# A recurrence with side work between its steps: the period of the side work reordered over three periods, and its pieces dealt out by number

## The chip, the cores and the metric

The kernel runs on one core of a Trainium2 chip. Its time is the device time of one execution in microseconds (us); the value quoted for a kernel is the median of several executions. The profiled execution is one more execution, recorded instruction by instruction; its own time and its span (first to last instruction) stand beside the median in the table below.

## The reference

Two layers are applied to x of 16 x 512 x 256 (batch B, time T, channels C), each an attention-like part and a feed-forward part, each followed by a residual and a layernorm:

```
x = layernorm(x + attention(x))          # 16 heads, latent size 32, causal softmax
x = layernorm(x + fp4_feed_forward(x))   # 704 wide, inputs and weights rounded to a 4-bit grid
x = layernorm(x + recurrence(x))         # the stage of this change
x = layernorm(x + time_mix(x))           # and of this change
# recurrence, after an RMS norm to xn, per head (state 64, input 16):
state = tanh(state @ tanh(a) + xn_t @ b)
mixed = state @ c + skip * xn_t          # then tokens + mixed @ w_out + b_out
# time_mix: xk, xr = mixes of x_t and x_(t-1)
out = sigmoid(xr @ W_r) * (relu(xk @ W_k)**2 @ W_v)
```

The recurrence is serial over the 512 time steps; everything else is not.

## The kernel before

The first stage does attention and the fp4 feed-forward, batch by batch. It ends at about 1830 us of the span. The second stage (L830 onward) does recurrence and time mix. It is one loop over t = 0..511 (L1167 on, with the TensorE order written out by hand: the program order is the queue order on PE). The other engines' queues are ordered by the framework, roughly in the order in which the code issues the work.

A step t of the loop has a fixed part:

- `advance_state(0, t)` (L1051): 8 small matmuls on PE (L1060; the profile's rows count them as x8) of group 0's last state with tanh(a), accumulated on the inputs that already lie in the PSUM tile `u`, then two tanh on ACT (L1068), which write the new state into the ring `hist`.
- `make_inputs(t)` (L1151, its matmuls L1020): 8 matmuls of a later step's xn with b, into a `u` tile (three such tiles; a new one is begun at t%4==0).
- **slot A**: side work may be issued here.
- `advance_state(1, t)`: the same for group 1.
- at t%8==7, copies of the last eight states from `hist` into `c` (POOL L1194 and L1198, DVE L1201).
- **slot B**: side work may be issued here.

A group's matmuls of step t+1 need the tanh of its step t. The side work belongs to blocks of 16 steps x 16 batches (32 blocks). A block's side work is cut into generators, each resumed piece by piece (`step`, L1118):

- N (`normed`, 2 pieces): the first loads x, squares and sums on DVE (L859), and scales on POOL (L863 to L867), with nothing on PE; the second turns it by four PE transposes (L883, `ps_xn`) and stores xn on DVE (L872).
- R (`read_out`, 2 pieces): 8 matmuls each from `c` (L1036, `ro`), then DVE L1045 into `ot`.
- A (`out_of_recurrence`, 4 pieces of 4 matmuls, L904, `ps_a`): loads `xm` and adds the bias on POOL (L909); after the last piece DVE adds the residual (L921), takes the layernorm's sums (L91, L92), POOL makes the factor (L84, L86), and DVE scales in two halves (L891).
- M (`mixes`, 1 piece): four transposes of A's result (L883, `ps_x`), then on DVE a copy (L934), a difference (L938) and the two mixes (L942, `muk`, `mur`); POOL keeps the last token (L935, L933).
- K (`key`, 4 pieces of 4 matmuls, `ps_k`): reads `muk`; then DVE relu (L958), POOL square (L959).
- G (`gate`, 4 pieces, `ps_rr`): reads `mur`; then two tanh on ACT (L975).
- V (`value`, 4 pieces, `ps_kv`): reads K's and G's results, then DVE L990, L991, the sums, POOL's factor, DVE L891 into `o`, and two DMAs out (L999).
- D (feed-forward of the last batch, 7 pieces, only in periods 0 and 1).

Each generator takes one of two PSUM banks for its products (`mm`), which is free again when its reader on DVE or ACT is done.

`PERIOD` is the order of a period of 16 steps; the number is the block's distance from the period (K-2 in period M works on block M-2). `TIME` holds a cost for each letter. The pace is the sum of the period's costs divided by 15.5; slot A of each step adds 0.3 of it to a budget and slot B 0.7, and pieces are issued while the budget is above zero. With these numbers a full period of 21 pieces falls out like this (slot A | slot B, "-" is empty; N0 and N1 are N's two pieces):

```
0 K0|N0 K1   1 -|K2   2 K3|G0   3 -|G1   4 -|G2   5 G3|R0   6 -|R1   7 -|A0
8 -|A1   9 A2|A3   10 -|N1   11 -|V0   12 V1|-   13 M|-   14 V2|V3   15 -|-
```

After t = 511 the work that is left of the last blocks runs without the recurrence ("the end").

Of the kernel before, what the change touches and what calls it, by code (L numbers as in the profile page):

```python
# [59 lines left out]
def tile_kernel(ctx: ExitStack, tc: tile.TileContext, I: dict, out: bass.AP):  # L60
# [196 lines left out]
    def vector_step():  # L257
        if vector_work:
            if next(vector_work[0][1], True):
                vector_work.pop(0)  # L260
# [80 lines left out]
    with ExitStack() as a:  # L341
# [319 lines left out]
        def step(name, args):  # L661

            if (name, args) not in tasks:
                tasks[name, args] = TASKS[name](*args)
            return next(tasks[name, args])

        def plan(b):
            todo = []
            for entry in {0: PLAN_0, 1: PLAN_1, B - 1: PLAN_15}.get(b, PLAN):
                c, *rest = entry[1:].split(".")  # L670
                todo.append((entry[0], (b + int(c), *map(int, rest))))
            return todo


        TIME = {"L": 0.86, "H": 1.7, "V": 0.9, "O": 0.9, "Q": 0.0, "U": 1.7, "D": 1.65, "W": 0.82, "P": 0.5}

        class Beside:
            def __init__(self, b):
                self.todo = plan(b)
                self.pace = sum(TIME[n] for n, _ in self.todo) / (4 * len(BLOCKS) * 8)  # L680
                self.left = 0.0
# [104 lines left out]
        with tc.manual_schedule(engines={mybir.EngineType.PE}):  # L786
            slots = [(b, g, n) for b in range(B) for g in range(4) for n in range(len(BLOCKS))]
            pTs, before, beside = [], None, None

            behind = []  # L790
            for slot in slots + [None]:
                if slot:
                    b, g, n = slot
                    if g == 0 and n == 0:
# [4 lines left out]
                        beside = Beside(b)  # L799
# [212 lines left out]
    def inputs(u, g, t0, n):  # L1012

        for k in range(2):
            for par in range(2):
                at = (t0 - g * 4) % RING + par
                for half in range(2):
                    for r in range(2):
                        rs, bs = slice(r * 64, r * 64 + 64), half * 32 + r * 16
                        nc.tensor.matmul(  # L1020
                            u[rs, k, par:n:2, bs : bs + 16],
                            wb[:, g * 2 + k, par, half, rs], xt[:, g, at : at + n - par : 2, :],
                            start=par == 0 and half == 0, stop=False, skip_group_check=True,
                        )
                yield
# [25 lines left out]
    def advance_state(g, t):  # L1051
        t0, _, u = us[g]
        if state[g] is not None:

            for k in range(2):
                own = state[g][:, k, :].rearrange("p (r s b) -> p r s b", r=2, s=2)
                into = u[:, k, t - t0, :].rearrange("p (s r b) -> p s r b", s=2, r=2)
                for c in range(2):
                    cs = slice(c * 64, c * 64 + 64)
                    nc.tensor.matmul(  # L1060
                        into[cs, :, c, :], ta[:, t % 2, g * 2 + k, cs], own[:, :, c, :],
                        start=False, stop=True, skip_group_check=True,
                    )
        state[g] = hist[g][t // 8 % 2][:, t % 8, :, :]
        with tc.high_priority():
            for r in range(2):
                rs = slice(r * 64, r * 64 + 64)
                nc.scalar.activation(  # L1068
                    state[g][rs, :, r * 32 : r * 32 + 32].rearrange("p k (s b) -> p k s b", s=2),
                    u[rs, :, t - t0, :]  # L1070
                    .rearrange("p k (s r b) -> p k s r b", s=2, r=2)[:, :, :, r, :],
                    AF.Tanh,
                )

    def beside(M):

        todo = [("N", 1)] * 2 if M == 0 else []
        for e in PERIOD:
            i = M + int(e[1:])
            if 0 <= i < T // TS:  # L1080
                todo.append((e[0], i))
        return todo + LATER.get(M, [])
# [1 line left out]


    PERIOD = [
        "K-2", "N2", "K-2", "K-2", "K-2", "G-2", "G-2", "G-2", "G-2", "R-1", "R-1", "A-1", "A-1",
        "A-1", "A-1", "N2", "V-2", "V-2", "M-1", "V-2", "V-2",
    ]


# [10 lines left out]
        ],  # L1102
    }

    TIME = {
        "E": 0.0, "F": 0.0, "N": 0.3, "K": 0.46, "G": 0.46, "R": 0.5, "A": 0.46, "V": 0.46, "M": 0.6,
        "U": 0.6, "D": 0.47,
    }
    KIND = {
        "N": normed, "K": key, "G": gate, "R": read_out, "A": out_of_recurrence, "V": value, "M": mixes,  # L1110
        "U": lambda j: ffn_up(B - 1, j), "D": lambda j: ffn_down(B - 1, j),
# [13 lines left out]
    with tc.manual_schedule(engines={mybir.EngineType.PE}):  # L1125
        for e in FIRST:
            end = False
            while not end:
                step(e[0], int(e[1:]))
                end = ends[0]  # L1130
        banks[:] = [ps_2]
        five.close()
        ps_u = ctx.enter_context(tc.tile_pool(name="ps_u", bufs=3, space=PSUM))

        copier[0] = nc.vector.tensor_copy
        product_of[0] = by_64
        us, ahead = [None, None], {}

        starts = [
            [(t0, 8) for t0 in range(0, T, 8)],  # L1140
            [(0, 4)] + [(t0, min(8, T - t0)) for t0 in range(4, T, 8)],
        ]
        pieces = []
        for g in range(2):
            for t0, n in starts[g]:
                for q in range(4):
                    pieces.append((t0 - 4 + q, g, t0, n))
        pieces.sort(key=lambda e: (e[0] if e[2] else -9, e[1], e[2]))
        making = {}

        def make_inputs(until):  # L1151
            while pieces and pieces[0][0] <= until:
                _, g, t0, n = pieces.pop(0)
                if (g, t0) not in making:
                    u = ps_u.tile([P, 2, 8, 64], F32, tag="u", name="u")
                    making[g, t0] = (u, inputs(u, g, t0, n))
                next(making[g, t0][1])

        todo, left, pace = [], 0.0, 0.0

        def some(more):
            nonlocal left
            left += more
            while left > 0 and todo:
                left -= step(*todo.pop(0))

        for t in range(T):  # L1167
            if t % 16 == 0:
                for e in todo:
                    step(*e)  # L1170
                todo, left = beside(t // 16), 0.0
                pace = sum(TIME[n] for n, _ in todo) / 15.5
                for g in range(2):
                    clean[t // 16, g] = histc.tile([P, 16, 2, 2, B], F32, tag=f"c{g}", name=f"c{g}")
            if t == 0:
                make_inputs(-1)
            for g in range(2):
                if us[g] is None or us[g][0] + us[g][1] == t:
                    t0, n = starts[g].pop(0)
                    us[g] = t0, n, making.pop((g, t0))[0]  # L1180
            vector_step()
            advance_state(0, t)
            make_inputs(t)
            some(pace * 0.3)
            advance_state(1, t)
            if t % 8 == 7:
                at = t % 16 - 7
                for g in range(2):
                    old, new = hist[g][t // 8 % 2], clean[t // 16, g]
                    old = old.rearrange("p t k (r s b) -> p t k r s b", r=2, s=2)  # L1190
                    for r in range(2):
                        rs, qs = slice(r * 64, r * 64 + 64), slice(64 - r * 64, 128 - r * 64)

                        nc.gpsimd.tensor_copy(  # L1194
                            new[rs, at : at + 8 : 2].rearrange("p t k s b -> p t k (s b)"),
                            old[rs, 0::2, :, r].rearrange("p t k s b -> p t k (s b)"),
                        )
                        nc.gpsimd.tensor_copy(  # L1198
                            new[rs, at + 1 : at + 8 : 2, :, r, :], old[rs, 1::2, :, r, r, :]
                        )  # L1200
                        nc.vector.tensor_copy(  # L1201
                            new[qs, at + 1 : at + 8 : 2, :, r, :], old[rs, 1::2, :, r, 1 - r, :]
                        )
            some(pace * 0.7)
        for e in todo:
            step(*e)
        for M in range(T // 16, T // 16 + 4):
            for e in beside(M):
                step(*e)
# [91 lines left out]
```

## Time and profile before

| what | value |
|---|---|
| median of 3 executions | 2583.96 us (2583.03 to 2585.3) |
| profiled execution, its own time | 2582.77 us |
| its span | 2581.0 us |
| mean granted TensorE clock | 0.983 |
| first state tanh (L1068) starts | 1830.4 us |
| last state tanh starts | 2549.1 us |

The second stage is thus the last 750 us of the span, 719 us of them the loop. In the profile's rows a matmul on PE has a weight load on PEld ahead of it; a row such as `L1060 MATMUL u<-hist,ta ... x8` is one `advance_state`. A number in brackets at the end of a row is the time that the engine was idle before it, with what ended the idle time. Times are us from the span's start, unless marked ns.

The start of every 64th L1068 row (4 per step, 16 steps) marks the periods. Period 0 takes 28.83 us, period 1 27.79, period 2 22.19, periods 3 to 29 take 22.08 on average (596.14 together), period 30 22.08, and the 15 steps of period 31 that are followed by another step 20.97.

### The profile page before, as it was taken

What the parts mean: (1) busy time and instruction counts of PE and PEld (TensorE: products, weight loads), DVE (VectorE), ACT (ScalarE), POOL (GpSimd) and SP (SyncE); (2) the same over time, 40 slices, a digit from 0 to 9 for tenths busy, and PEclk for the clock granted to TensorE, in tenths of its full rate; (3) what the DMA queues carried; (4) which work ended last, traced back from release to release, by engine and by line L of the source; (5) the groups of instructions that cost most, each with busy time, mean ns of one, the idle gap of its engine ahead of it and who ended that gap; (6) DMA issues with size and microseconds to landing.
All of it is one profiled execution on the core that took longest, in us unless ns stands there. A gap on an engine that the chain in (4) does not pass through costs nothing.

```text
span 2581.0 us, 73861 instructions
## 1 busy us (share of the span) xinstructions
PE 2438.0 (94%) x28802; PEld 1715.8 (66%) x28802; DVE 1946.9 (75%) x5621; ACT 1615.6 (63%) x5532; POOL 1048.2 (41%) x1649
## 2 busy tenths in 40 slices
PE   8789999999999999999999999996899999999997
PEld 4456666666666666666666666664677777777775
DVE  6767888787887888878888788887566666666665
ACT  4656666666666666666666666753366666666663
POOL 4322333333333333333333333333555555555653
PEclk9899999999999999999999999998899999999999
DMA  3000000000000000000000000000101111111100
GB/s 118 22 10 5 22 13 16 13 15 16 19 14 16 15 12 23 14 16 15 12 24 14 15 15 4 15 14 9 49 29 40 37 38 40 40 38 37 35 28 22
DMA packets 58016, 61.30 MB, mean 24 GB/s; under 512 B 7873, under 2 KB 53058, under 8 KB 57666
## 3 DMA queue, kind: packets, MB, share of 16 engines
q1 hardware_dynamic: 56802, 55.54, 6.9%
q8 instruction: 226, 3.70, 0.6%
q10 hardware_dynamic: 864, 1.05, 0.1%
q14 instruction: 124, 1.02, 0.1%
HBM read 39.79 MB, written 16.78 MB: 22 GB/s over the span
## 4 chain that ended last, share of the span: by engine, by line
PE 58%; DVE 27%; ACT 7%; POOL 4%; issue 3%; DMA 0%; ACTq 0%; POOLq 0%; DVEq 0%; SPq 0%
PE u L1060 7%; PE ps_pt L559 6%; PE S L524 5%; DVE p L536 5%; PE u L1020 4%; PE pg L160 4%; PE pu L160 3%; PE py L590 3%; ACT p L549 3%; PE ps_h L439 3%; PE ps_d L160 2%; PE ps_a L904 2%; PE ps_k L904 2%; ACT pT L561 2%; PE ps_q L457 2%
## 5 line engine op out<-in xcount | busy, mean ns | idle before, releaser
L549 ACT ACTIVATE p<-p,nm 128x512 f32<-128x512 f32 (+3 forms) x1024 | 569.7, 561 | 520.8 <-DVE nm L536 516.7
L1068 ACT ACTIVATE hist<-u 64x64 f32<-64x64 f32 x2048 | 447.3, 218 | 250.8 <-PE u L1060 182.5
L536 DVE CUSTOM_DVE_ANT_0 p<-S,mask 128x512 f32<-128x512 f32 (+3 forms) x1024 | 443.7, 483 | 50.1 <-PE S L524 50.1
L559 PEld LDWEIGHTS ps_pt<-ident,p 128*128 128x128 f32 x2560 | 296.7, 141 | 235.5 <-issue 86.2
L1060 PEld LDWEIGHTS u<-hist,ta 128*64 128x64 f32 x8176 | 362.9, 138 | 121.0 <-ACT hist L1068 41.6
L559 PE MATMUL ps_pt<-ident,p 128*128 128x128 f32 x2560 | 393.6, 280 | 9.2 <-DVE nm L536 3.5
L561 ACT COPY pT<-ps_pt 128x384 f32<-128x384 f32 (+1 forms) x768 | 370.3, 515 | 38.9 <-PE ps_pt L559 38.6
L1060 PE MATMUL u<-hist,ta 128*64 128x32 f32 x8176 | 384.2, 219 | 4.8 <-ACT hist L1068 4.5
L214 POOL TENSOR_TENSOR q_q<-q_q,q_m 128x256 f32<-128x256 f32 (+1 forms) x142 | 168.7, 1188 | 457.0 <-DVE q_q L213 442.7
L524 PE MATMUL S<-kc,qr 32*128 32x128 f32 (+3 forms) x2048 | 235.7, 474 | 8.9 <-ACT qr L478 7.9
L1020 PE MATMUL u<-xt,wb 128*64 128x64 f32 x4128 | 223.2, 230 | 3.5 <-issue 2.4
L549 ACT ACTIVATION_READ_ACCUMULATOR p<-p,nm 128x1 f32 x1024 | 198.9, 194 | 0.0
L160 PE MATMUL pg<-wgT,xqT 128*128 128x352 f32 x512 | 177.5, 470 | 4.2 <-ACT xqT L289 2.9
L473 POOL TENSOR_TENSOR qc<-qc,qs 128x512 f32<-128x512 f32 x64 | 81.6, 1275 | 236.0 <-DVE qs L472 230.9
L160 PE MATMUL pu<-wuT,xqT 128*128 128x352 f32 x512 | 172.5, 459 | 1.2 <-DVE th L304 1.2
L160 PE MATMUL ps_d<-wdT,hT 128*128 128x256 f32 x732 | 169.5, 381 | 2.2 <-ACT hT L323 2.2
L1020 PEld LDWEIGHTS u<-xt,wb 128*64 128x64 f32 x4128 | 165.0, 139 | 9.4 <-issue 3.0
L590 PEld LDWEIGHTS py<-pT,vpad 128*32 128x32 f32 x5120 | 141.2, 110 | 43.2 <-issue 30.7
L590 PE MATMUL py<-pT,vpad 128*32 128x128 f32 x5120 | 165.3, 276 | 3.8 <-ACT pT L561 3.5
L524 PEld LDWEIGHTS S<-kc,qr 32*128 32x128 f32 x2048 | 111.0, 185 | 78.2 <-issue 32.0
L160 PEld LDWEIGHTS ps_d<-wdT,hT 128*128 128x128 f32 x732 | 134.8, 191 | 19.6 <-ACT hT L323 3.1
L84 POOL TENSOR_SCALAR ve<-mv 128x1 f32<-128x1 f32 (+1 forms) x160 | 32.8, 205 | 264.5 <-DVE mv L92 234.7
(164 smaller groups left out, 4620.4 us busy)
## 6 DMA issues: line engine op xcount, KB each, us to landing
xT<-in_xT_dram SPq DMA_DIRECT2D x16, 512.0 KB
x<-in_x_dram SPq DMA_DIRECT2D x16, 512.0 KB
xs<-x SPq DMA_DIRECT2D x64, 128.0 KB
x<-xs SPq DMA_DIRECT2D x32, 256.0 KB
xm<-xs SPq DMA_DIRECT2D x32, 256.0 KB
out_dram<-o SPq DMA_DIRECT2D x64, 128.0 KB
w<-in_w_down_dram SPq DMA_DIRECT2D x2, 352.0 KB
w<-in_w_gate_dram SPq DMA_DIRECT2D x5, 128.0 KB
```

The source lines that it names most:

```text
L160: nc.tensor.matmul(dst, left, right, start=start, stop=stop)
L214: nc.gpsimd.tensor_tensor(q, q, m, ALU.subtract)
L524: nc.tensor.matmul(S[h][:, at : at + w], q[rs, i * P : i * P + P], k[rs, :w], start=True, stop=True,)
L536: nc.vector.tensor_tensor_reduce(out=p[:, own], in0=S[h][:, own], in1=mask[:, T - (i + 1) * P :], scale=1.0, scalar=-MASKED, op0=ALU.add, ...
L549: nc.scalar.activation(p[:, own], p[:, own], AF.Exp, bias=nm[:, u : u + 1], scale=-1.0, accum_out=sum_of[b, g][:, cb, half, h : h + 1],)
L559: nc.tensor.transpose(ps[:, at : at + P], p[:, at : at + P], ident)
L561: nc.scalar.copy(pT[:, :w], ps[:, :w])
L590: nc.tensor.matmul(py[q * 32 : q * 32 + 32, PLACE[i][1], :], vpad[b % 2][:, j, g * 4 + h, :], pt, start=j == 0 and h % 2 == 0, stop=j == i ...
L904: nc.tensor.matmul(dst[cs], left[:, cs], right, start=first, stop=not first)
L1020: nc.tensor.matmul(u[rs, k, par:n:2, bs : bs + 16], wb[:, g * 2 + k, par, half, rs], xt[:, g, at : at + n - par : 2, :], start=par == 0 an ...
L1060: nc.tensor.matmul(into[cs, :, c, :], ta[:, t % 2, g * 2 + k, cs], own[:, :, c, :], start=False, stop=True, skip_group_check=True,)
L1068: nc.scalar.activation(state[g][rs, :, r * 32 : r * 32 + 32].rearrange("p k (s b) -> p k s b", s=2), u[rs, :, t - t0, :] .rearrange("p k ( ...
```

## The change

The order of the period changes, V moves from two to three blocks behind, and the costs in `TIME` are gone: pieces are counted. At step k of a period of n pieces, `left` is n - n*(k+1)//16; slot A issues pieces while more than left + 1 remain, slot B until `left` remain. `step` returns N's first piece as 0.0, so that `piece` goes on behind it, if the count allows.

```diff
     PERIOD = [
-        "K-2", "N2", "K-2", "K-2", "K-2", "G-2", "G-2", "G-2", "G-2", "R-1", "R-1", "A-1", "A-1",
-        "A-1", "A-1", "N2", "V-2", "V-2", "M-1", "V-2", "V-2",
+        "N2", "V-3", "V-3", "V-3", "V-3", "K-2", "K-2", "R-1", "R-1", "K-2", "K-2", "A-1", "A-1",
+        "A-1", "A-1", "G-2", "G-2", "G-2", "G-2", "N2", "M-1",
     ]
...
-        todo, left, pace = [], 0.0, 0.0
-
-        def some(more):
-            nonlocal left
-            left += more
-            while left > 0 and todo:
-                left -= step(*todo.pop(0))
+        todo, number = [], 0
+
+        def piece(left):
+
+            while len(todo) > left and not step(*todo.pop(0)):
+                pass
...
-                todo, left = beside(t // 16), 0.0
-                pace = sum(TIME[n] for n, _ in todo) / 15.5
+                todo = beside(t // 16)
+                number = len(todo)
...
             make_inputs(t)
-            some(pace * 0.3)
+
+            left = number - number * (t % 16 + 1) // 16
+            while len(todo) > left + 1:
+                piece(left + 1)
             advance_state(1, t)
...
-            some(pace * 0.7)
+            piece(left)
```

A full period now falls out like this:

```
0 -|N0   1 -|V0   2 -|V1   3 V2|V3   4 -|K0   5 -|K1   6 R0|R1   7 -|K2
8 -|K3   9 A0|A1   10 -|A2   11 -|A3   12 G0|G1   13 -|G2   14 -|G3   15 N1|M
```

Period 2 has no V yet (17 pieces), periods 30 and 31 have no N (19 pieces), and period 1 has 16 pieces: N0, R0, R1, A0 to A3, N1, M, D0 to D6, one to a step. Period 0 has N0 and N1 of blocks 1 and 2 and fourteen D pieces; before, those four N pieces stood in slot A of steps 0 and 1, and now they stand in slot B of steps 0 to 3. In the order of the PE queue, behind the last step's matmuls, now stand M of block 30, V29, half of K30, R31, the rest of K30, A31, G30, M31, V30, K31, G31, V31; before, K30, G30, R31, A31, half of V30, M31, the rest of V30, K31, G31, V31.

More of the change, by code (lines that the diff above doesn't have):

```diff
@@ L1102, in tile_kernel @@
         ],
[L1103 to L1107, printed above, removed]
     }
```

## Prediction

> **What bounds the kernel now.** I read the page first, then the busy time by stretches of the second stage, then the waits of PE inside the loop, then the timeline of single periods.
>
> ```profile
> span 2581.0 us, 73861 instructions
> PE 2438.0 (94%) x28802; PEld 1715.8 (66%) x28802; DVE 1946.9 (75%) x5621; ACT 1615.6 (63%) x5532; POOL 1048.2 (41%) x1649
> ...
> 1830.00:1859.00 29.00, 25.25 (x485) 20.95 (x483) 14.90 (x41) 13.90 (x64) 22.16 (x33) 0.82 0.15 43
> 1859.00:1887.00 28.00, 23.38 (x468) 18.95 (x466) 13.34 (x38) 14.10 (x66) 11.32 (x29) 0.88 0.09 26
> 1909.00:2505.00 596.00, 584.31 (x12748) 471.38 (x12744) 401.33 (x1033) 395.23 (x1782) 344.15 (x752) 1.00 0.13 38
> 2549.00:2581.00 32.00, 16.89 (x130) 9.69 (x126) 18.29 (x46) 1.61 (x6) 8.64 (x17) 0.80 0.09 25
> ```
>
> The stretches' columns are length, then busy time of PE, PEld, DVE, ACT, POOL, the granted clock, the DMA share and GB/s. In the full periods (1909 to 2505) PE is busy 98% at full clock; periods 0 and 1 and the end have PE holes and a low clock. So a change of order can win only what is left of PE's waits. In 1909 to 2505 PE waits, by name, for this:
>
> ```profile
> PE ps_x L883 <- DVE x L891: 7.0, 21, 0.6
> PE u L1060 <- ACT hist L1068: 4.0, 26, 0.2
> ```
>
> The first is M waiting for A's layernorm. Period 17 (from 2218.62) has the wait, period 18 (from 2240.76) has not:
>
> ```profile
> 2231.41 0.63 PE L904 MATMUL ps_a<-woutT,ot 128*64 128x256 f32 x4
> 2235.27 1.70 DVE L891 TENSOR_SCALAR x<-x,mv,rstd 128x256 f32<-128x256 f32 x2 [0.80 <-POOL rstd L86]
> 2235.44 1.38 POOL L909 TENSOR_TENSOR xm<-xm,bout 128x512 f32<-128x512 f32 x1 [0.20 <-DMA xm<-xs]
> 2236.30 0.44 PE L883 MATMUL ps_x<-ident,x 128*128 128x128 f32 x2
> 2237.02 0.44 PE L883 MATMUL ps_x<-ident,x 128*128 128x128 f32 x2 [0.29 <-DVE x L891]
> ...
> 2257.41 0.74 DVE L891 TENSOR_SCALAR x<-x,mv,rstd 128x256 f32<-128x256 f32 x2 [0.68 <-POOL rstd L86]
> 2258.41 0.66 PE L883 MATMUL ps_x<-ident,x 128*128 128x128 f32 x4
> 2259.22 1.28 POOL L909 TENSOR_TENSOR xm<-xm,bout 128x512 f32<-128x512 f32 x1 [1.85 <-DMA xm<-xs]
> ```
>
> In period 17 POOL's L909 starts before the second half of L891, and the two halves take 1.70 instead of 0.74 us; M's second half waits. In period 18 L909 comes later, M's four transposes run together. Period 17 takes 22.14 us, period 18 takes 21.61: M's wait costs **0.53**. Periods 8, 11, 21 and 25 are like 18 (21.61 each), period 28 nearly (21.71), the rest of 3 to 29 like 17 or longer; their mean is 22.08.
>
> **The change, part by part.** *Work per step.* From the starts of PE's rows in period 17: an advance of a group holds PE 0.20, the inputs 0.26, a product piece 0.44 to 0.47. So a step without a piece is 0.67 of PE work, with one 1.12, with two 1.56. By the starts of L1068 the step with one piece in slot B takes 1.13 and with two 1.55 to 1.57 (PE's work), but the empty step 15 takes 1.05: there the chain advance, tanh, advance is the limit, and 0.37 is lost. R, N and M hold PE 0.24 to 0.27 longer than a product. The new full period has again five steps with two pieces, ten with one, and one without PE work (step 0 in place of step 15). The count therefore buys **nothing** in a full period: same rows, same holes. A new `u` tile costs about 0.17 at steps 4 and 12 in both orders, since slot B of the step ahead is full in both.
>
> *M's wait.* A3 to M was 4.9 us (2231.41 to 2236.30). Now slot B of step 11 to slot B of step 15 is steps 12 (1.56 + 0.17), 13 and 14 (1.13 each) and N1 ahead of M in step 15 (0.67 + 0.7 + 0.17 for the rest): 5.6 us. A's chain needs 5.6 in the slow form (2231.41 to 2237.02) and 4.6 without L891's excess of 0.96. L909 is now queued on POOL between the history copies of steps 14 and 15, behind A's factor (L86), so it cannot hold L891. M's data wait goes: 22.08 becomes 21.61.
>
> *What is late next: M's bank.* In the new order M takes the bank that G has just left, one step earlier, and so waits for G's second tanh. The nearest rows are these of period 16:
>
> ```profile
> 2203.04 0.60 PE L904 MATMUL ps_rr<-wrT,mur 128*64 128x256 f32 x4
> 2203.69 0.38 ACT L975 ACTIVATE th<-ps_rr 128x256 f32<-128x256 f32 x1 [0.17 <-PE ps_rr L904]
> 2203.97 0.51 ACT L1068 ACTIVATE hist<-u 64x64 f32<-64x64 f32 x2
> 2204.51 0.39 ACT L975 ACTIVATE th<-ps_rr 128x256 f32<-128x256 f32 x1
> ```
>
> The second tanh ends 1.86 after G3's start. From G3's start to M: 0.44 + 0.20 + 0.26 + 0.7 (N1) + 0.3 = 1.9. So between 0 and one more state pair (0.5) if that gets ahead; I take 0.05, as the rows' order on ACT is the same in the new program (tanh, state pair, tanh). Behind M on PE stands the next step's advance, so this wait would be paid in full. Full periods 3 to 29: 27 x (22.08 - 21.66) = **-11.3**.
>
> [...] Around steps 15 and 0 POOL now has eight history copies (0.35 to 0.45 each), L909 (1.28) and the carry, and on DVE at the same time stand M's difference and mixes and N's squares, and K0 waits for the first mix. [...] By the rows the loss is smaller: L942's pair took 1.20 beside L867 at 2239.02 and 0.87 in the quiet end, L938 1.22 beside L909 at 2259.83 and 0.69 elsewhere. [...] I take the rows: cost nothing. Other slacks are larger: R1 to A0 3.4 us for 1.5 of work, K3 to G0 4.2 for 1.4, A3 to N1 4.9 for 1.4, V3 to R0 (bank) 3.2 for 1.4.
>
> *N0's and V's queues.* N0's load, V's two output DMAs and `xm`'s load keep their order of one each a period on SP, and `x` and `xm` are loaded a period or more ahead; no wait there reaches PE. V one block later holds th, ka and x three buffers deep at most; the reuse is ten steps away.
>
> *Period 0.* N1's transposes waited for POOL's xn in slot A of steps 0 and 1 (3.2 us on PE, 1832 to 1837). xn comes at the same time, but PE then stands in step 3, two steps further: two bare steps (1.34) and the two empty steps 9 and 15 (0.75) fall away. **-2.1**, between 0 and -4.
>
> *Period 1* (27.79). M waits for A's factor, which POOL makes behind history copies:
>
> ```profile
> 1873.55 1.08 PE L883 MATMUL ps_x<-ident,x 128*128 128x128 f32 x4 [3.94 <-DVE x L891]
> ```
>
> After it the clock is 0.53 (stretch 1873 to 1879). The new period adds up to 1.05 (N0) + 2 x 1.39 (R) + 10 x 1.13 + 1.5 (D0's transposes) + 2 x 1.41 (N1, M) + 0.33 = 19.8, and waits of 0.7 (R on copies), 0.5 (D1 on hT) and about 2.5 for M, since A3 and M now stand a step later against the copies of step 7, which are further done when M asks. At full clock 23.5. [...] By the rule 23.5, by the row 25.5. I take between: **-3.0** (0 to -4.5).
>
> *Period 2* has four V pieces less: 4 x 0.44 and M's wait, **-2.3**. *Periods 30 and 31*: no N, no empty step, no wait of M (0.6 and 1.3 there): about 20.4 against 22.08, and 18.6 + 0.4 against 20.97 for what stands ahead of the last state: **-1.6, -2.0**.
>
> *The end* gets M30, V29 and half of K30 more. They lie in the 5 us in which R31 waits for the history copies and DVE anyway (it started 5.0 after the last advance); M30's chain puts R31 at about 5.5. After A31 G30 fills PE, and L990 no longer stands between d and `muk`, so 0.7 comes back. **-1.0** (-2 to +1.5).
>
> Sum: -2.1 - 3.0 - 2.3 - 11.3 - 1.6 - 2.0 - 1.0 = -23.3. The profiled execution's own time is 2582.77 (span 2581.0, 1.8 around it): 2559.5. The median lies 1.2 above that execution: **2560.7**.
>
> **Rivals.** *The wait is handed on (0.12).* M waits for G's tanh by a state pair more, 0.45 in each of 27 periods: the gain there is gone and about 12 remain from the edges: 2572. For it: G3 to M is one step where 1.9 is needed and 1.9 is there. Against: ACT is 66% busy.
>
> *K0 waits for `muk` (0.05), slower.* [...]
>
> *The change acts only at the edges and not on M (0.06)*, because A's chain is slow again in the new place: -12 and some loss, 2572 to 2579.
>
> *The edges give more (0.10)*: full clock in periods 0 and 1, 2553.
>
> **How the numbers follow.** The likeliest case (0.67) is 2560.7, its own range 2554 to 2568. The range 2552 to 2575 takes in the handed-on wait and the better edges, and leaves out the slower rival. About 0.2% (5 us) is what a measurement of this kernel can tell from no change. Faster by more: 0.67 + 0.12 + 0.10 and half of the third rival (0.03), less 0.03 of the likeliest for steps misjudged: 0.89; within: the other half and 0.02 of these, 0.05; slower: 0.05 and 0.01, 0.06.
>
> **What would show it.** Right: no row in periods 3 to 29 with M waiting for L891; periods of 21.6 to 21.7; L891 at 0.74 for its two halves everywhere; period 2 under 20. [...] It would be most wrong if a full period had a wait that I placed under a slack.

## The result, and the profile after

The changed kernel takes 2561.18 us (median of 4 runs, 2558.65 to 2561.73), the kernel before 2583.49 beside it (2581.19 to 2585.3): a ratio of 0.9912, 95% interval 0.99 to 0.9924. The forecast was 2560.7. The profiled execution of the changed kernel took 2558.65 with a span of 2556.6, against 2582.77 and 2581.0 before.

The head of the changed kernel's page:

```profile
span 2556.6 us, 73922 instructions
PE 2428.8 (95%) x28802; PEld 1713.3 (67%) x28802; DVE 1944.7 (76%) x5621; ACT 1613.2 (63%) x5532; POOL 1036.7 (41%) x1649
```

Its busy time by stretches, which are periods 0, 1, 3 to 29, and the end; columns as before (length, busy PE, PEld, DVE, ACT, POOL, granted clock, DMA share, GB/s):

```profile
1829.00:1855.00 26.00, 23.08 (x482) 19.09 (x479) 18.55 (x42) 13.49 (x62) 21.41 (x34) 0.93 0.17 48
1855.00:1881.00 26.00, 22.79 (x463) 18.59 (x462) 13.39 (x37) 14.15 (x66) 10.99 (x28) 0.87 0.10 28
1901.00:2486.00 585.00, 580.70 (x12758) 472.03 (x12756) 395.00 (x1036) 393.80 (x1782) 337.13 (x752) 1.00 0.13 38
2525.00:2557.00 32.00, 19.00 (x176) 11.40 (x172) 21.59 (x53) 3.35 (x13) 10.08 (x21) 0.90 0.09 25
```

The full periods are 11 us shorter at nearly the same count of PE rows, and PE is busy 99% of them. What PE still waits for in 1901 to 2486:

```profile
PE u L1060 <- ACT hist L1068: 4.1, 27, 0.2
PE ps_x L883 <- ACT th L975: 0.2, 1, 0.2
```

M's 21 waits for L891 are gone; the state's wait, one in each period (the step without a piece), is what it was. One M of 27 shows a wait for G's second tanh. The neighbourhood of M in one full period of the changed kernel (start, length, engine, line, operation; in brackets the idle time ahead and what ended it):

```profile
2222.43 0.73 DVE L891 TENSOR_SCALAR x<-x,mv,rstd 128x256 f32<-128x256 f32 x2 [1.09 <-POOL rstd L86]
...
2223.97 1.27 POOL L909 TENSOR_TENSOR xm<-xm,bout 128x512 f32<-128x512 f32 x1
...
2223.98 0.66 PE L883 MATMUL ps_xn<-ident,xn 128*128 128x128 f32 x4
2224.25 1.41 DVE L1199 COPY c<-hist 64x128 f32<-64x128 f32 x2 [1.09 <-ACT hist L1068]
2224.49 0.38 ACT L975 ACTIVATE th<-ps_rr 128x256 f32<-128x256 f32 x1
...
2224.92 0.66 PE L883 MATMUL ps_x<-ident,x 128*128 128x128 f32 x4
```

A's layernorm (L891) is through at 2223.16 with two halves of 0.73 together, 1.76 ahead of M. POOL's bias add L909 comes 0.8 after it. It now lies beside a history copy on DVE instead: two L1199 take 1.41, where their median is 0.31 each; nobody on PE asks for that copy then, and the DVE work queued behind it reaches PE in time. G's second tanh ends at 2224.87 and M starts at 2224.92, 0.05 behind it; in all 27 full periods it is 0.05 to 0.07.

Where the span's 24.4 us went, by the starts of every 64th L1068 (us; the three columns on the right are experiments told below):

| stretch | forecast | before | changed | difference | order alone | before, no bias add | changed, no bias add |
|---|---|---|---|---|---|---|---|
| up to the first state | 0 | 1830.37 | 1829.62 | -0.75 | 1832.18 | 1830.71 | 1831.33 |
| period 0 | -2.1 | 28.83 | 26.15 | -2.68 | 27.61 | 24.82 | 25.06 |
| period 1 | -3.0 | 27.79 | 25.62 | -2.17 | 27.12 | 27.84 | 24.14 |
| period 2 | -2.3 | 22.19 | 19.91 | -2.28 | 20.74 | 21.60 | 19.92 |
| periods 3 to 29 | -11.3 | 596.15 | 584.79 | -11.36 | 583.88 | 583.55 | 585.26 |
| period 30 | -1.6 | 22.08 | 21.19 | -0.89 | 21.26 | 22.06 | 20.70 |
| period 31 | -2.0 | 20.97 | 18.38 | -2.59 | 19.77 | 20.95 | 18.39 |
| the end | -1.0 | 32.62 | 30.92 | -1.70 | 30.18 | 30.63 | 30.93 |

### The profile page after: what moved, and what is told of

Same layout as the page of the kernel before. It is cut to its first block, busy times and chain, and to the rows that moved or that the text cites. A ratio compares the mean times of both kernels' runs of the same rounds, so it can differ in the third digit from the quotient of the medians.

```text
span 2556.6 us, 73922 instructions
## 1 busy us (share of the span) xinstructions
PE 2428.8 (95%) x28802; PEld 1713.3 (67%) x28802; DVE 1944.7 (76%) x5621; ACT 1613.2 (63%) x5532; POOL 1036.7 (41%) x1649
## 3 DMA queue, kind: packets, MB, share of 16 engines
q10 hardware_dynamic: 864, 1.05, 0.1%
## 4 chain that ended last, share of the span: by engine, by line
PE 54%; DVE 28%; ACT 9%; POOL 5%; issue 3%; DMA 1%; ACTq 0%; DVEq 0%; POOLq 0%
PE u L1060 8%; DVE p L536 6%; PE ps_pt L559 5%; PE u L1020 5%; PE S L524 4%; ACT p L549 4%; PE py L590 3%; PE pg L160 3%; PE pu L160 3%; PE ps_h L439 3%; ACT pT L561 3%; DVE q_q L207 2%; PE ps_a L904 2%; PE ps_d L160 2%; DVE q_sc L201 2%
## 5 line engine op out<-in xcount | busy, mean ns | idle before, releaser
L1068 ACT ACTIVATE hist<-u 64x64 f32<-64x64 f32 x2048 | 445.5, 218 | 235.1 <-PE u L1060 153.0
L1060 PE MATMUL u<-hist,ta 128*64 128x32 f32 x8176 | 394.2, 218 | 4.6 <-ACT hist L1068 4.4
```

What stands on the lines that cost most here:

```text
L1060: nc.tensor.matmul(into[cs, :, c, :], ta[:, t % 2, g * 2 + k, cs], own[:, :, c, :], start=False, stop=True, skip_group_check=True,)
L1068: nc.scalar.activation(state[g][rs, :, r * 32 : r * 32 + 32].rearrange("p k (s b) -> p k s b", s=2), u[rs, :, t - t0, :] .rearrange("p k ( ...
```

## The experiments

The theory: in the old order POOL's L909 lies beside A's layernorm, L891 is held, and M waits for it; the new order takes M and L909 out of each other's way, and the dealing by number brings nothing in a full period. The rivals: the dealing evens the steps and carries the gain; or M simply stood too near to A, with L909 a bystander.

**The order alone.** The kernel before with only this edit:

```
-        "K-2", "N2", "K-2", "K-2", "K-2", "G-2", ... "N2", "V-2", "V-2", "M-1", "V-2", "V-2",
+        "N2", "V-3", "V-3", "V-3", "V-3", "K-2", "K-2", "R-1", "R-1", ... "G-2", "N2", "M-1",
```

> The new order of the period, dealt out by the old rule of costs and pace. M then stands in slot B of step 14, A's last piece in slot B of step 9, G's last in slot B of step 12, and the step without a piece is step 15 as before. Theory (the order takes M away from A's chain, the dealing is worth nothing in a full period): M's wait for L891 is gone, full periods of 21.6 to 21.7 as in the changed kernel, time 2559 to 2566, the spread being the edges, where the two dealings put the pieces differently. Rival (the dealing by number carries the gain, for it evens the steps): full periods stay at 22.0 to 22.1, time 2575 to 2583.

Measured: 2564.68, ratio 0.9924 (0.991 to 0.9938). Full periods of 21.61, no M row waiting. The order carries the whole gain of the full periods (583.88, even 0.9 under the changed kernel). Periods 0, 1, 2 and 31 are 1.46, 1.50, 0.83 and 1.39 longer than in the changed kernel, the end 0.74 shorter: the dealing by number is worth some 4 us in this order, and at the edges only. (This is read from the periods of two profiled executions; the intervals of the two ratios overlap.)

**The dealing alone.** The changed kernel with the old `PERIOD`.

> The old order of the period, dealt out by number. M stands in slot B of step 14 and A's last piece in slot B of step 11: from the one to the other are about 3.8 us, where A's chain needs 4.6 without a hold and 5.6 with one. Theory: M waits for L891 0.8 to 1.8 in every period and its restart adds to it, full periods of 22.4 to 23.4, time 2592 to 2620, slower than before. Rival (the dealing by number carries the gain): full periods under 22.0, time under 2578.

Measured: 2626.77, ratio 1.0164 (1.015 to 1.0177): slower than before, and by more than expected. The sign was right and the wait was the wrong one. The profile shows no gap ahead of M: L891's halves take 0.41 or less, from A's last piece to M go 4.4 and not the 3.8 expected, and M starts at most 0.2 before the second half ends. It is K0 that waits. The waits of PE in its full periods (us in total, times, longest), and then the rows of one period:

```profile
PE ps_k L904 <- DVE muk L942: 32.5, 24, 1.7
PE u L1060 <- ACT hist L1068: 0.3, 1, 0.3
```

```profile
2161.88 0.66 PE L883 MATMUL ps_x<-ident,x 128*128 128x128 f32 x4
2162.69 0.68 DVE L934 COPY x3T<-ps_x 128x512 f32<-128x512 f32 x1
2163.10 1.27 POOL L909 TENSOR_TENSOR xm<-xm,bout 128x512 f32<-128x512 f32 x1
2163.40 1.05 DVE L1199 COPY c<-hist 64x128 f32<-64x128 f32 x1
2164.49 0.77 DVE L938 TENSOR_TENSOR d<-x3T 128x512 f32<-128x512 f32 x1
2165.29 0.31 DVE L1199 COPY c<-hist 64x128 f32<-64x128 f32 x1
2165.63 0.94 DVE L942 SCALAR_TENSOR_TENSOR muk<-d,cols,x3T 128x256 f32<-128x256 f32 x2
...
2166.20 0.65 PE L904 MATMUL ps_k<-muk,wkT 128*64 128x256 f32 x4 [1.28 <-DVE muk L942]
```

M has moved to step 14 and K0 is the first piece of step 0, 3.0 us behind it; from M's start to K0's, which stands right behind the first half of `muk` that it asks for, go 4.3. In that chain stands one history copy that L909 holds to 1.05 instead of 0.31; these 0.74 are the larger part of the 1.28 that K0 waits here, and the rest is the short distance itself. My expectation counted M's distance to A and forgot to count K0's to M. So the wait that the forecast named as its slower rival exists where the distance is too short, 1.35 each time. What the other DVE instructions between M and K0 take longer is at most a small part of it: L938 takes 0.77 here against 0.69 elsewhere, L859 0.61 against 0.42. The changed kernel has 6.34 from M to K0 (2224.92 to 2231.26 in the period shown above), and K0 does not wait.

A full period of the dealing alone takes 23.82, 1.7 more than before, and a part of that is the clock: in seven of the 27 periods the granted clock falls to 0.50 for 3.41 us behind K0's wait, and these periods take 24.9 to 25.1, the others 23.0 to 23.8.

**The kernel before without the bias add**, and **the changed kernel without it**: one line taken out of each, so that the output bias is missing from the result.

```
-        nc.gpsimd.tensor_tensor(x, x, bout.unsqueeze(1).to_broadcast([P, 2, C]), ALU.add)
```

> The kernel before without POOL's bias add L909: the output bias is left out of x. Order and dealing are untouched. Theory (L909 beside L891's second half holds it, and that alone makes M wait in the old order): L891 takes 0.4 each everywhere, no M row waits for it in the full periods, periods of 21.6 in place of 22.1, about 21 x 0.53 = 11 less: 2572 to 2574. Rival (M simply stands too near to A's chain in the old order, and L909 is a bystander): the wait and the 22.1 stay, 2581 to 2584.

> The changed kernel without L909, the output bias left out as in the kernel before without it. Theory: in the new order L909 holds nothing that PE waits for, so full periods stay at 21.6 to 21.65 and the time within 1.5 of the changed kernel, 2560 to 2562. If L909 still cost the new order something in period 1 or at the end, it would show as 2 to 3 us less there.

Measured: 2565.96 (0.9926, 0.9913 to 0.9938) and 2558.23 (0.9898, 0.9883 to 0.9913). What the rows of L891 for `x` look like in the full periods of before, of before without L909, and of the changed kernel (durations in ns: least, median, greatest), in this order:

```profile
L891 DVE TENSOR_SCALAR x<-x,mv,rstd x54: 401/415/1487, 1925.8 to 2500.2; 128x256 f32<-128x256 f32 x54
```

```profile
L891 DVE TENSOR_SCALAR x<-x,mv,rstd x54: 405/412/415, 1921.6 to 2483.9; 128x256 f32<-128x256 f32 x54
```

```profile
L891 DVE TENSOR_SCALAR x<-x,mv,rstd x54: 407/410/416, 1919.3 to 2482.8; 128x256 f32<-128x256 f32 x54
```

One POOL instruction, taken out of a kernel whose order is untouched, takes the long halves of 1.49 away, and with them M's wait: full periods of 21.60, 12.6 less over 27 of them, a little more than the new order brings. The bystander theory is out. And the two do not add up: in the new order L909 is worth nothing in the full periods (585.26 against 584.79). Both the new order and the missing add remove one and the same wait. The rest of the first kernel's gain (6 to 8 us more than expected) lies in period 0 (-4.0), period 2 (-0.6) and the end (-2.0). In period 0 L909 costs in another way: before, two of them stand on POOL for 2.50 us, from 1823.73, ahead of the xn that N's transposes wait for, and without them these waits fall from 3.2 to 1.2. The changed kernel without the add is 3.0 under the changed kernel's 2561.18, but the intervals of the two ratios overlap, and the changed kernel run once more (below) took 2558.11; in the profiled executions period 1 is 1.5 and period 0 1.1 shorter than in the first trace of the changed kernel, period 1 only 0.9 than in the second (25.05). The expectation had allowed for period 1 alone.

**A third tanh.** To see what the 0.05 between G's second tanh and M are worth, the changed kernel with that tanh issued twice:

```
         for i in range(2):
             nc.scalar.activation(th[:, i, :], ps[:, i * C : i * C + C], AF.Tanh, scale=0.5)
+        nc.scalar.activation(th[:, 1, :], ps[:, C : 2 * C], AF.Tanh, scale=0.5)
```

> The changed kernel with G's second tanh issued twice (one more ACT instruction of 0.38 in each period, the same result). In the changed kernel M started 0.05 after that tanh's end, in the bank that it frees. Theory (the wait is handed on to the tanh as soon as these 0.05 are gone, and is paid in full since the next step's advance stands behind M): M waits 0.3 to 0.35 in each full period and restarts for up to 0.2 more, 27 x 0.33 to 0.55 = 9 to 15 more, 2570 to 2576. Rival (the bank's release is not what M stands at, or the hole of the step behind takes the wait up): no M row that waits for the tanh, 2560 to 2564.

Measured: 2563.6 (0.9933, 0.992 to 0.9947). The wait is there as worked out, in every period:

```profile
PE ps_x L883 <- ACT th L976: 7.8, 27, 0.3
PE u L1061 <- ACT hist L1069: 4.2, 27, 0.2
```

One of them, by its rows:

```profile
2232.00 0.38 ACT L976 ACTIVATE th<-ps_rr 128x256 f32<-128x256 f32 x1
...
2232.44 0.66 PE L883 MATMUL ps_x<-ident,x 128*128 128x128 f32 x4 [0.28 <-ACT th L976]
```

M starts 0.05 to 0.06 behind the third tanh in every period, the same as behind the second in the changed kernel. So the 0.05 there are the lag from a tanh's end to M's start and no slack: counted from the start of the advance ahead of M, the last tanh ends 0.35 later (0.65 against 0.30), and M starts 0.35 later too (0.71 against 0.36). The waits are 0.29 each, and with the restart step 15 is 0.41 longer (2.44 against 2.03). But the full period is only 0.2 longer (21.83): steps 1, 4, 9 and 12 are shorter by 0.06 to 0.09 each, step 7 longer by 0.06. So the handed-on wait is real and half of it is given back within the period. What gives it back no run here tells; "paid in full" was wrong.

**N's first half not counted as a piece.** N's first half issues no PE work, and the step that holds it is the one without any. The changed kernel with:

```
                 todo = beside(t // 16)
+                if todo and todo[0][0] == "N":
+                    step(*todo.pop(0))
                 number = len(todo)
```

> The changed kernel with N's first half (it issues no PE work) stepped at the period's start and not counted as a piece: 20 pieces on 16 steps, four steps with two pieces, twelve with one, none without PE work. Theory (the step without a piece is bound by the chain advance, tanh, advance, takes 1.03 where its PE work is 0.67, and so loses 0.37 that pieces can fill): a full period becomes 21.25 to 21.35 from 21.63, some 28 x 0.33 = 9 less, 2550 to 2554. K0 then stands at the end of step 3, about 4.9 behind M, where muk's chain took 5.06 in the changed kernel: K0 may wait up to 0.15 a period. Rival (that chain bounds the loop as such, and the loss comes back in other steps): full periods stay at 21.6, 2560 to 2562. The slower rival of the prediction (K0 waits for muk because POOL holds DVE there): K0 waits over 0.5 a period and nothing is won.

Measured: 2559.58 (0.9916, 0.9903 to 0.993): nothing won. Neither theory named the cause. The state's wait is gone from PE's list, K0 does not wait, and a new one stands there:

```profile
PE ps_kv L904 <- POOL c L1198: 5.0, 13, 0.6
PE ps_kv L904 <- DVE xt L872: 3.0, 10, 0.3
```

V's first piece is now the first of step 0, right behind N and M. Product tiles take turns between two banks (L148), so V takes the bank that N's transposes fill, and must wait until DVE's L872 has emptied it. The rows of one period:

```profile
2204.27 1.41 DVE L1201 COPY c<-hist 64x128 f32<-64x128 f32 x2 [1.30 <-ACT hist L1068]
...
2205.71 0.88 DVE L872 TENSOR_SCALAR xt<-ps_xn,cols 128x256 f32<-128x256 f32 x2
...
2206.73 0.65 PE L904 MATMUL ps_kv<-wvT,ka 128*64 128x256 f32 x4 [0.32 <-DVE xt L872]
```

N's transposes ended at 2204.66, but L872 started only behind the two history copies, of which L909 holds one, and ended at 2206.59; V started 0.14 later. (Where the list names L1198, V stands 0.14 behind L872's end too; it is a POOL copy that ended about then.) Step 0 takes 1.58 on average where 1.13 was expected, which eats the gain: full periods of 21.71. In the changed kernel the step without a piece covers this wait: V mostly starts 0.7 behind L872's end there.

**The same with M ahead of N.** Then V takes the bank that M leaves, and N the one that waits for G's tanh:

```
-        "A-1", "A-1", "G-2", "G-2", "G-2", "G-2", "N2", "M-1",
+        "A-1", "A-1", "G-2", "G-2", "G-2", "G-2", "M-1", "N2",
```

> As the kernel in which N's first half is no piece, with M ahead of N's second half at the period's end: M starts about 0.9 earlier in the period, in A's bank, and N takes the bank that G leaves. Theory: L891 ends 1.7 before M in the changed kernel, so 0.8 are left and M does not wait; K0 is 0.9 further from M and loses what it may wait in the other kernel; full periods 21.2 to 21.3, equal to it or up to 4 less, 2548 to 2553. Rival (A's chain stands at its edge and M's wait for L891 comes back as soon as M goes earlier): M waits 0.3 to 0.8, full periods of 21.6 to 22.1, 2560 to 2575.

Measured: 2555.55 (0.9898, 0.9884 to 0.9912). Full periods of 21.43, V's wait all but gone, and M does not wait for L891 in them: it still starts 1.0 behind L891's end, so A's chain has the 0.9 to spare. Step 0 is still 1.30. In period 1, where A is late, M's wait grew from 3.1 to 4.5 and the period took 29.2; that is why the total shows less than the 6.2 that the full periods won.

**M later in period 1.** The kernel with N's first half uncounted, and in period 1 four D pieces ahead of N and M:

```
+        if M == 1:
+            at = len(todo) - 9
+            todo[at:] = todo[at + 2 : at + 6] + todo[at : at + 2] + todo[at + 6 :]
```

> As the kernel in which N's first half is no piece, and in period 1 four of the seven D pieces stand ahead of N's second half and M. Theory (period 1 holds one wait of M for L891 of 3.1, in which L909 beside L891 is about 1, and after it a half clock that costs 1 to 2): M finds its data, no clock below 1.00 in period 1, period 1 takes 20.5 to 22 in place of 25.6, so 3.5 to 5 less than the kernel without that edit, 2546 to 2550. Rival (the stall of period 1 is the pipeline's filling and moves to another piece, D's hT or K0's muk): less than 1.5 won.

Measured: 2555.91 (0.9901, 0.9887 to 0.9914). Period 1 takes 21.65 in place of 25.94, D waits 1.2 once and M only 0.2, for its bank; period 2 stays at 19.55. The stall was M's place and not the filling of the pipeline. The edit won 3.7 against the kernel without it, inside the 3.5 to 5 expected; the total missed its 2546 to 2550 because that kernel had won nothing.

**Both**, and **both with three bare steps at the start of period 0** (`number * max(0, t - 2) // 13` for the first sixteen steps), run beside the changed kernel once more.

> M ahead of N's second half, N's first half no piece, and in period 1 four of D's pieces ahead of M and N. Theory (the gains lie in different periods and add up): full periods of 21.4 as in the kernel with M ahead of N, period 1 near the 21.65 of the kernel with M later there in place of 29.2, so 2546 to 2550, the fastest of all. Rival (what period 1 wins is lost in period 2, where K0 stands nearer behind M): period 2 over 21 in place of 19.55, 2551 to 2555.

> As the kernel with both, and in period 0 the first three steps have no piece; its pieces are dealt out to the other thirteen. Theory (N's transposes come before POOL's xn in the first steps, 1.2 to 1.8 of wait and a half clock after it): period 0 takes 24 to 25 in place of 25.4 to 26.2, 0.5 to 2 less than the kernel with both. Rival (the data of period 0 comes from POOL's quantization at its own pace, and a later start only pushes the wait into D1's pieces): the same time within 1, or up to 2 more.

> The changed kernel once more, beside the two kernels built on it: 2557 to 2563. It gives the distance of both to it on one chip.

Measured: 2547.23 (0.9865, 0.9849 to 0.9882), 2547.23 (0.9862, 0.9848 to 0.9877) and 2558.11 (0.9906, 0.9891 to 0.9921). The gains add up: period 1 at 21.57, full periods at 21.42. Both are about 11 us under the changed kernel on one chip. The full periods of the kernel with both:

```profile
1898.00:2476.00 578.00, 577.26 (x12736) 476.66 (x12734) 388.55 (x1036) 393.70 (x1782) 331.31 (x751) 1.00 0.13 39
```

PE is busy 577.26 of 578 us. An order of pieces can win nothing more there by ending waits of PE, but the work is not at its least either: step 0 still takes 1.30. The bare start won 0.4 in period 0 and nothing in the total: the wait for `xn` fell from 1.7 to 0.3, and D's wait for `hT` rose from 1.4 to 2.7, with 1.2 more for the bank ahead of it, as the rival had it.

## Why the prediction was right, step by step

*The bound.* Right: what was won in the full periods was PE's wait. Of 11.4 us, 7.0 are the waits for L891 themselves. The rest goes with M's restart: its four transposes take 0.66 in one go, and 0.44 twice with the gap between them, 21 x 0.22 = 4.6 by these rows. Over the two stretches shown PE's busy time fell by 3.6 and its idle time by 7.4.

*The count buys nothing in a full period.* Right, shown by the order alone: 21.61 a period in most, as good as the 21.63 of the changed kernel. It left out that the dealing is worth some 4 us at the edges in the new order.

*M's wait, 0.53 a period, made by L909 beside L891.* Right, and shown by taking L909 out of the kernel before. 22.08 became 21.66, as forecast. From A3 to M the trace has 5.96; the step said 5.6, and its own terms add up to 5.5. It was on the safe side: with M 0.9 earlier it still finds its data.

*M's bank, 0.05.* Right in place: M starts with no slack behind G's second tanh (G3 to M takes 1.97, the step had 1.9), and the profile shows one wait of 0.2 in 27 periods. That the mean came to 21.66, as 21.61 and 0.05 do, is partly luck: most full periods take 21.63 and four of them 21.70 to 21.89. That such a wait "would be paid in full" was wrong by half.

*K0 and `muk`, taken at no cost.* Right for this placement: from M's start to `muk` go 5.06 in the changed kernel (2224.92 to 2229.98, both halves), and K0, 6.34 behind M, does not wait. L938, with two inputs, took 0.69 beside the carry copies L935 and L933, as it does elsewhere. The long holds in the full periods of before all stand beside L909, whether the DVE instruction has one input or two: L891 and N's squares L859, up to 1.49 against 0.41, and M's difference L938, three times 1.19 to 1.36 against 0.69. L909 is not alone in this: with the dealing alone V's L891 takes up to 1.17 beside POOL's square L959 of about 1.1. The distance is needed all the same: the dealing alone shows K0's wait as soon as M stands 3 us ahead of it.

*Period 0*, -2.1 against -2.68, and *period 2*, -2.3 against -2.28: right in size.

*Period 1*, -3.0 against -2.17: the term that was the most mis-sized for its weight. Two parts of it. M's wait was taken as 2.5 and was 3.05, since here L909 lies beside L891 again, which the step did not look for:

```profile
1867.87 1.26 POOL L909 TENSOR_TENSOR xm<-xm,bout 128x512 f32<-128x512 f32 x1
1867.94 1.66 DVE L891 TENSOR_SCALAR x<-x,mv,rstd 128x256 f32<-128x256 f32 x2 [0.23 <-POOL rstd L86]
...
1869.34 1.12 PE L883 MATMUL ps_x<-ident,x 128*128 128x128 f32 x4 [3.05 <-DVE x L891]
```

Without L909 that wait is 2.2 and the period 24.14. And the clock did fall: M's transposes at 1869.34 take 1.12 instead of 0.66, and the granted clock is 0.50 in 1869 to 1872. Of the two values between which I went, 25.5, by the row, was right (25.62, and 25.05 in the second trace). The rule for the 23.5 no run shows: in period 1 the granted clock fell to 0.53 in the kernel before (1873 to 1879) and to 0.50 in the changed kernel.

*Period 30*, -1.6 against -0.89: V's first piece waits 0.3 there for the bank that N left, since period 30 has no N first half and so no step without a piece. It is the same wait that the kernel with N uncounted shows in nearly every period, and without L909 period 30 takes 20.70. The forecast's list of slacks had the bank that V leaves and not the one that it takes. *Period 31*, -2.0 against -2.59, and *the end*, -1.0 against -1.70: right in sign, somewhat small. Another 0.75 of the profiled executions' difference lies ahead of the second stage, which the change does not touch. So the edges' sum is right partly by luck: it was 12.0, and 12.3 came, with period 1 and period 30 short by 0.8 and 0.7 and period 0, period 31 and the end over by 0.6, 0.6 and 0.7. From the profiled execution to the median 1.2 was added, as before; in the changed kernel it is 2.5, which hides that the profiled execution itself came out 0.85 under the forecast's 2559.5.

*The rivals.* Handed on to the tanh: M did come to stand at the tanh with nothing to spare, but a state pair did not get ahead, and the 0.45 a period did not come. K0 waiting for `muk`: not here; the wait is shown with the old order dealt by number, and there in the main through a history copy that L909 holds to 1.05 in place of 0.31. Only the edges: no, the edges gave 12 and the full periods 11.4. The edges giving more with a full clock: the clock rose from 0.82 to 0.93 in period 0, and not in period 1 (0.88 and 0.87).

## What to carry to other kernels

When an engine that is nearly always busy waits at one place in each period, look at which instruction made the producer late in the slow periods and not in the fast ones; here it was a POOL add that nobody waited for, and moving the consumer was worth 0.42 us a period and removing the add 0.47, but the two do not add up. Before filling an empty slot in such a loop, list what the slot covered: here the release of one of two banks, and the fill won only once the order handed over the banks in another way. And when pieces move, count each moved piece's distance to its producer and to its consumer; with only one of the two counted, the forecast of one experiment had the wrong wait.

## What the runs showed of the hardware that I had not expected

The add on POOL holds a DVE copy as it holds the layernorm's scaling (L891, up to 1.49 against 0.41 in the kernel before): L1199, with one input, has a median of 0.31 us and reached 1.27 in the full periods of the changed kernel; without L909 its greatest is 0.38.

The granted clock fell to 0.50 behind waits of PE of 0.83 and 0.63, and stayed at 1.00 behind one of 1.24. Period 0 of the kernel with both edits, six microseconds a row; in the first row PE waits 0.83 and 0.63 for `xn`, in the second 0.20:

```profile
1830.00:1836.00 6.00, 4.45 (x113) 3.80 (x114) 6.00 (x16) 1.76 (x9) 5.46 (x8) 0.98 0.11 34
1836.00:1842.00 6.00, 5.80 (x70) 4.75 (x70) 4.42 (x7) 2.05 (x10) 4.58 (x4) 0.50 0.18 59
```

With the bare start PE waits 0.28 and 1.24 in the second row, and the clock stays at 1.00 there and in the six microseconds behind:

```profile
1830.00:1836.00 6.00, 5.21 (x147) 4.97 (x148) 5.97 (x16) 3.27 (x15) 5.56 (x7) 1.00 0.02 5
1836.00:1842.00 6.00, 4.34 (x77) 3.18 (x75) 5.13 (x9) 2.39 (x11) 5.82 (x5) 1.00 0.28 88
```

So 1.55 of idle in short pieces (6.00 less 4.45) went ahead of a half clock, and 1.66 (6.00 less 4.34) with a longer piece did not. Ahead of these rows PE stood idle once more in both kernels, for 2.44 from 1827.49 in the first and for 2.43 from 1828.26 in the second; the first kernel's waits lie closer behind it, and that may count.

The dealing alone has no such neighbour. K0 waits 1.0 to 1.7 once in each of its full periods. The granted clock is at 0.50 for 3.41 us behind seven of these waits, of 1.15 to 1.70, and stays at 1.00 behind the others, of up to 1.62. The seven falls lie 47.79, 71.68 or 95.57 apart, which are 14, 21 and 28 times 3.413. In the loop of the changed kernel, too, the stretches at one granted clock are 3.413, 23.893, 6.827 and 675.839 long, which are 1, 7, 2 and 198 times that. So in these traces the clock seems to be set at times of a grid of its own, and not at each wait; what of the idle time then decides, these runs leave open.
